# A perceiver block: the last batch's self-attention in two halves of heads, its early routing in quarters of the array, and the experts' residual on VectorE

## The chip, the cores and the metric

The kernel runs on one core of a Trainium2 chip. A core has five engines that run side by side and wait for each other through semaphores: TensorE (PE in the profile; PEld is its loading of weights), VectorE (DVE), ScalarE (ACT), GpSimd (POOL) and SyncE (SP, which here only issues DMAs). The metric is the device time of one execution in microseconds (us), lower is better.

## What is computed

Sixteen batches of 128 rows by 512 columns go through cross-attention to 2048 context rows, self-attention with 16 heads of 32 (causal, half of each head rotated), and a layer of 8 experts of which the first row of each batch chooses two. In short:

```
x = x + softmax(LN(x) ctx^T) ctx                     # cross-attention, LN = layernorm
h = LN(x); q, k, v = h Wq, h Wk, h Wv                # per head, q and k rotated
x = x + (softmax(q k^T * scale + causal) v) Wc       # self-attention
h = LN(x); gates = softmax over the top 2 of h[0] Wr^T
x = x + h + sum over the 2 experts of gate_e * (h A_e^T) B_e^T
```

All data are float32. The choice of experts needs only row 0 of the layernorm after self-attention, and row 0 attends only to itself (the mask is causal), so that its attention output is its own v.

## The kernel before

The kernel is written as four generators per batch, each cut into steps by `yield`, and an order of steps written out by hand.

- `score(b)` (line 260): the first layernorm, its transposes, the scores against the context (`psc`), their maximum (`mx`), the exponentials and sums.
- `attend(b)` (line 323): the weighted sum over the context (`av`), four groups of products; then `x1` and the second layernorm.
- `inner(b)` (line 345): transposes of the layernorm (`hT`), the v projection (`project`), k and q with their rotation (`rotated`, `turned`), `kb` (k spread over a block per head), the comparison (`compare`, products `pss`), softmax in four groups of four heads (`weigh`), the transposed probabilities `pT`, the products with v (`y`, copied to `yT`), and the output projection (`o`), which gives `x2` and the third layernorm.
- `experts(b)` (line 598): transposes (`hT`), the residual `res = x2 + h`, the routing (`shares`, `route`, `gates`), then `mid` and `ffn` and the output.

`early(b)` (line 563) computes the routing of the last batch ahead, from row 0 alone: its v (`v0`), its output row (`o0`), its layernorm, the logits. `route` (line 517) ends in GpSimd's indirect DMAs, which gather the two chosen experts' weights: two into `each` and one into `wb`; GpSimd then copies `each` into `wa`. `each` has one buffer, and so has `res`.

TensorE executes in exactly the order in which the steps issue its products. On VectorE, ScalarE and GpSimd a planner orders the instructions, except for those marked `pinned`, which keep the written order among themselves. All queues run in order once planned.

The main loop (line 708) treats batches 0 to 13. In one round it interleaves `inner(b)`, the score of b + 2, the attend of b + 1 and the experts of b - 1. Transposes go through DRAM there by way of SyncE's queue; the context is loaded through ScalarE's queue, outputs leave through GpSimd's. Lines 756 to 791, after the loop, hold the order of the last two batches, y = 14 and z = 15, whose probabilities are transposed on TensorE instead. In the rotation, VectorE shuffles pairs of rows (line 384), GpSimd multiplies by the sines (line 385), VectorE multiplies by the cosines (line 388) and adds (line 395). The addition reads two SBUF operands, and so does the residual on GpSimd (lines 606 and 608). The products with PE are recorded twice each (a float32 product of 128 columns is two records).

The program prints here what the change touches:

Of the kernel before, what the change touches and what calls it, by code (L numbers as in the profile page):

```python
# [38 lines left out]
C_MIXED = 392  # L39
C_N = 520  # L40
# [6 lines left out]
def constants():  # L47

    c = np.zeros((P, C_N), np.float32)
    c[:, C_MASK : C_MASK + P] = np.where(np.tril(np.ones((S, S), bool)), 0.0, NEG)  # L50
    c[:, C_MIXED : C_MIXED + P] = c[:, C_MASK : C_MASK + P].reshape(P, QD, 4).transpose(0, 2, 1).reshape(P, P)
    inv = (1.0 / np.float32(10000.0) ** (np.arange(0, DE, 2, dtype=np.float32) / DE)).astype(np.float32)
    freqs = np.arange(S, dtype=np.float32)[:, None] * inv[None, :]
    emb = np.concatenate((freqs, freqs), axis=-1)


    cos, sin = np.ones((DH, S), np.float32), np.zeros((DH, S), np.float32)
    cos[DE:] = np.cos(emb).T
    sin[DE:] = np.sin(emb).T * np.tile(np.array([-1.0, 1.0], np.float32), DE // 2)[:, None]
    c[:, C_COS : C_COS + S] = np.tile(cos, (4, 1))  # L60
    c[:, C_SIN : C_SIN + S] = np.tile(sin, (4, 1))
    c[:, C_BLK : C_BLK + 2] = np.arange(P)[:, None] // 32 % 2 == np.arange(2)[None, :]
    at = np.arange(P)
    c[:, C_ONE], c[:, C_TWO] = at < R, at >= R
    c[:, C_ONER], c[:, C_TWOR] = R * (at < R), R * (at >= R)
    c[:, C_RANK], c[:, C_P] = at % R, at
    return c
# [3 lines left out]
def perceiver_block(ctx: ExitStack, tc: tile.TileContext, io: dict, out: bass.AP):  # L71
# [19 lines left out]
    nc.gpsimd.memset(mhalf, -0.5)  # L91

# [252 lines left out]
    def inner(b):  # L345
# [27 lines left out]
        def rotated(n, t):  # L373

            ps = bank(ps_acc, "acc", f"{n}_{b}")
            for m in range(HC):
                for c in range(KC):
                    matmul(
                        ps[:, m * P : (m + 1) * P].rearrange("p (a i) -> p a i", a=4),
# [3 lines left out]
            partner = p1.tile([P, HC, S], F32, tag="partner", name=f"{n}P_{b}")  # L383
            pinned(nc.vector.stream_shuffle(partner.rearrange("p c t -> p (c t)"), ps, PARTNERS))
            nc.gpsimd.tensor_tensor(  # L385
                partner, partner, cst[:, None, C_SIN : C_SIN + S].to_broadcast([P, HC, S]), ALU.mult
            )
            pinned(nc.vector.tensor_tensor(
                t, ps.rearrange("p (c t) -> p c t", c=HC),
                cst[:, None, C_COS : C_COS + S].to_broadcast([P, HC, S]), ALU.mult,  # L390
# [3 lines left out]
        def turned(n, t):  # L394
            pinned(nc.vector.tensor_tensor(t, t, turning[n], ALU.add))  # L395

        kbs, pss, turning = [], [], {}
# [3 lines left out]
        def blocked():  # L401

            turned("k", kT)
            kb = p1.tile([P, HC, 2, S], F32, tag="kb", name=f"kb_{b}")
            for half in range(2):

                nc.scalar.activation(  # L407
                    kb[:, :, half, :].rearrange("p c (q i) -> p c q i", q=4),
                    kT.rearrange("p c (i q) -> p c q i" if mixes else "p c (q i) -> p c q i", q=4),
                    AF.Copy, scale=column(C_BLK + half),  # L410
                )
            kbs.extend(kb[:, c] for c in range(HC))

        def compare():


            pss.extend(
                bank(pool, tag, f"pss_{b}_{tag}_{half}")
                for pool, tag in ((ps_sc, "sc"), (ps_acc, "acc")) for half in range(2)
            )  # L420
            for c, kb in enumerate(kbs):
                for half in range(2):
# [3 lines left out]
                        qT[of, c, :], kb[of].rearrange("p h t -> p (h t)"),  # L426
# [36 lines left out]
        parts += [lambda group=group: weigh(group) for group in range(4)]  # L463

        for part in [project] + parts if b < B - 1 else parts + [project]:
            part()
            yield

        if b >= B - 2:
            flat = att.rearrange("p h t -> p (h t)")  # L470
            for half in range(2):
                transposed(
                    flat[:, half * H // 2 * S : (half + 1) * H // 2 * S], pT[half],
                    f"p_{b}_{half}", True,
                )
                yield
        acc = bank(ps_acc, "acc", f"y_{b}")
        for c in range(HC):
            first = c // 2 * 8 + c % 2 * 2
            for j, n in enumerate((first, first + 1, first + 4, first + 5)):  # L480
                at = c * P + j * DH
                matmul(
                    acc[j * DH : (j + 1) * DH, c * P : (c + 1) * P].rearrange(
                        "p (a i) -> p a i", a=4
                    ),
                    vv[:, at : at + DH], pT[n // 8][:, :, n % 8, :], start=True, stop=True,
                )
        yT = p1.tile([P, HC, S], F32, tag="yT", name=f"yT_{b}")
        nc.scalar.copy(yT, acc.rearrange("p (c t) -> p c t", c=HC))
        yield  # L490
        acc = bank(ps_acc, "acc", f"o_{b}")
        for c in range(HC):
            matmul(acc, yT[:, c, :], w["c"][:, c, :], start=(c == 0), stop=(c == HC - 1))
        x2 = p2.tile([P, D], F32, tag="x2", name=f"x2_{b}")
        nc.vector.tensor_tensor(x2, acc, x1, ALU.add)  # L495
        lasts[b] = (x2, layernorm(x2, f"3_{b}", mix=b >= B - 2))
        yield
# [65 lines left out]
    def early(b):  # L563
# [11 lines left out]
        tr = bank(ps_tr, "tr", f"v0_{b}")  # L575
        for m in range(HC):
            for c in range(KC):
                matmul(
                    tr[:, m : m + 1], w["v"][:, c, m * P : (m + 1) * P], hT[:, 0, c, :1],
                    start=(c == 0), stop=(c == KC - 1),  # L580
                )
        v0 = small(b, KC, "v0")
        nc.vector.tensor_copy(v0, tr[:, :KC])
        yield
        acc = bank(ps_acc, "acc", f"o0_{b}")
        for c in range(KC):
            matmul(acc[:1, :], v0[:, c : c + 1], w["c"][:, c, :], start=(c == 0), stop=(c == KC - 1))
        row = p1.tile([1, D], F32, tag="row", name=f"row_{b}")
# [9 lines left out]
    def experts(b):  # L598
# [5 lines left out]
        res = p1.tile([P, D], F32, tag="res", name=f"res_{b}")  # L604
        if b < B - 2:
            pinned(nc.gpsimd.tensor_tensor(res, x2, h, ALU.add))
        else:
            nc.gpsimd.tensor_tensor(plain(res), plain(x2), mixed(h), ALU.add)
# [15 lines left out]
        nc.scalar.activation(mid, ps[:, :S], AF.Copy, scale=gate)  # L624
        yield
# [142 lines left out]
    step(attend, z)  # L768
    step(inner, y)
    step(attend, z)  # L770
    step(experts, y - 1)
    step(inner, y)
    step(experts, y - 1)
    step(inner, y)
    step(inner, z, 3)
    step(inner, y)
    step(inner, z, 2)
    step(inner, y)
    step(experts, y - 1, 2)
    step(inner, z, 5)  # L780
    step(early, z)
    step(inner, y)
    step(early, z)
    step(inner, z)
    step(experts, y)
    step(early, z)
    step(experts, y, 3)
    step(early, z)
    step(inner, z, 4)
    step(experts, y, 2)  # L790
    step(experts, z, 3)
# [43 lines left out]
```

## Time and profile before

| | |
|---|---|
| median of 3 runs | 845.15 us (843.19 to 848.23) |
| the profiled execution's own time | 850.18 us |
| its span in the profile | 848.1 us |
| PE busy | 809.2 us, 95% of the span |
| VectorE busy | 529.7 us, 62% |
| ScalarE busy | 258.0 us, 30% |
| GpSimd busy | 168.8 us, 20% |
| mean rate of the DMAs | 249 GB/s |
| one round of the loop | 48.83 us |
| last av product of batch 15 ends | 779.20 us |

The span is what lies between the first and the last instruction or transfer that the profile shows; the execution's own time has 2.1 us more around it. A line of a timeline gives start and duration in us, engine, line of the kernel, operation, output and inputs, their shapes, how many, and in brackets the idle time before it and what ended it. L95 is the helper that records every product, L98 the one for transposes, so products are told apart by the names of their tiles. The granted clock is a share of TensorE's full clock.

### The profile page before, as it was taken

The numbers are of one execution on the slowest core, as the hardware profiler recorded it, in microseconds if no ns is written. First come the engines' busy times: TensorE is split into PE (matmuls) and PEld (weight loads), VectorE is DVE, ScalarE is ACT, GpSimd is POOL, SyncE is SP. The second block draws the span as 40 slices with busy tenths as digits, with TensorE's granted clock in tenths as the row PEclk, the third lists the DMA queues.
The fourth block names the chain that finished last, engine by engine and source line by source line (L and its number), as shares of the span: only waits on it lengthen the run. The fifth ranks groups of instructions, "written<-read, shape, count | busy, mean of one in ns | idle before, by whom it ended". The sixth has DMA issues, their size and how long they took to land.

```text
span 848.1 us, 14295 instructions
## 1 busy us (share of the span) xinstructions
PE 809.2 (95%) x5514; PEld 575.3 (68%) x5514; DVE 529.7 (62%) x1204; ACT 258.0 (30%) x763; POOL 168.8 (20%) x232
## 2 busy tenths in 40 slices
PE   6999999999999999999999999999999999998985
PEld 6846775768677675868667576867757686774832
DVE  1454759395675849476584948668593966757541
ACT  1232324151232314133332413223241422324320
POOL 1001011222221212222211122222112222212232
PEclk9999999999999999999999999999999999999897
DMA  9998394958859495876949496684939578450101
GB/s 365 391 353 323 105 378 158 345 219 290 314 181 399 133 363 198 305 287 201 391 141 372 174 325 271 231 355 158 389 144 353 233 252 343 163 224 13 38 21 54
DMA packets 76739, 211.04 MB, mean 249 GB/s; under 512 B 6400, under 2 KB 42624, under 8 KB 60288
## 3 DMA queue, kind: packets, MB, share of 16 engines
q10 hardware_dynamic: 15696, 113.32, 33.5%
q1 hardware_dynamic: 56880, 84.23, 28.2%
q0 software_dynamic: 4096, 12.59, 4.5%
q8 instruction: 43, 0.70, 0.3%
q14 instruction: 24, 0.20, 0.1%
HBM read 180.23 MB, written 29.88 MB: 248 GB/s over the span
## 4 chain that ended last, share of the span: by engine, by line
PE 76%; DVE 14%; POOL 6%; issue 2%; ACT 1%; DMA 0%; DVEq 0%; POOLq 0%; ACTq 0%
PE psc L95 27%; PE av L95 21%; PE o L95 7%; PE v L95 7%; DVE sc L307 3%; DVE qT L395 3%; PE pss_sc L95 2%; POOL kP L385 2%; POOL qP L385 2%; PE y L95 2%; PE ffn L95 2%; PE mid L95 2%; PE pss_acc L95 2%; DVE st L127 1%; DVE x L495 1%
## 5 line engine op out<-in xcount | busy, mean ns | idle before, releaser
L95 PE MATMUL psc<-hT,ctxT 128*128 128x128 f32 x2048 | 237.8, 278 | 1.4 <-ACT hT L173 1.4
L95 PEld LDWEIGHTS psc<-hT,ctxT 128*128 128x128 f32 x2048 | 233.8, 194 | 2.5 <-ACT hT L173 2.0
L95 PE MATMUL av<-ctx,sc 128*128 128x512 f32 x512 | 227.1, 596 | 0.0
L95 PEld LDWEIGHTS av<-ctx,sc 128*128 128x128 f32 x512 | 94.6, 190 | 110.9 <-issue 109.9
L441 ACT ACTIVATE att<-att,nmx 128x128 f32<-128x128 f32 x256 | 98.7, 387 | 102.1 <-DVE nmx L439 102.1
L131 POOL TENSOR_SCALAR rs<-mv 128x1 f32<-128x1 f32 x48 | 11.2, 232 | 445.6 <-DVE mv L129 238.6
L282 ACT COPY sc<-psc 128x512 f32<-128x512 f32 x64 | 37.4, 585 | 139.6 <-PE psc L95 139.6
L310 ACT ACTIVATE sc<-sc 128x512 f32<-128x512 f32 x64 | 40.2, 630 | 90.9 <-DVE sc L307 90.4
L95 PE MATMUL o<-w_c,yT 128*128 128x512 f32 x128 | 61.6, 627 | 4.2 <-issue 4.2
L95 PE MATMUL k<-hT,w_k 128*128 128x128 f32 x512 | 61.6, 280 | 0.7 <-ACT hT L173 0.7
L95 PEld LDWEIGHTS k<-hT,w_k 128*128 128x128 f32 x512 | 60.1, 196 | 1.8 <-ACT hT L173 0.9
L95 PE MATMUL q<-hT,w_q 128*128 128x128 f32 x512 | 59.8, 275 | 0.0
L95 PE MATMUL v<-w_v,hT 128*32 128x512 f32 x512 | 58.7, 592 | 0.9 <-DVE w_v L229 0.9
L95 PEld LDWEIGHTS q<-hT,w_q 128*128 128x128 f32 x512 | 58.5, 192 | 0.0
L285 DVE TENSOR_TENSOR mx<-psc,mx 128x512 f32<-128x512 f32 x32 | 21.6, 676 | 57.3 <-ACT sc L282 57.3
L137 DVE TENSOR_SCALAR h<-x,mv,rs 128x512 f32<-128x512 f32 x48 | 28.2, 587 | 33.1 <-POOL rs L134 33.1
L441 ACT ACTIVATION_READ_ACCUMULATOR att<-att,nmx 128x1 f32 x256 | 47.9, 187 | 0.0
L407 ACT ACTIVATE kb<-kT,cst 128x512 f32<-128x512 f32 x32 | 35.7, 1164 | 37.8 <-DVE kT L395 37.8
L95 PEld LDWEIGHTS o<-w_c,yT 128*128 128x128 f32 x128 | 25.3, 208 | 29.9 <-issue 29.9
L495 DVE TENSOR_TENSOR x<-o,x 128x512 f32<-128x512 f32 x16 | 11.1, 692 | 54.8 <-PE o L95 54.8
L307 DVE TENSOR_TENSOR sc<-sc,spread 128x512 f32<-128x512 f32 x64 | 42.6, 672 | 3.3 <-PE spread L95 3.3
L285 DVE TENSOR_TENSOR mx<-psc,sc 128x512 f32<-128x512 f32 x16 | 11.1, 691 | 53.0 <-ACT sc L282 53.0
(127 smaller groups left out, 933.3 us busy)
## 6 DMA issues: line engine op xcount, KB each, us to landing
ctx<-in_ctx_dram ACTq DMA_DIRECT2D x56, 1024.0 KB
ctxT<-in_ctxT_dram ACTq DMA_DIRECT2D x52, 1024.0 KB
there_p<-pX SPq DMA_DIRECT2D x28, 512.0 KB
pT<-there_p SPq DMA_DIRECT2D x28, 512.0 KB
ctxT<-in_ctxT_dram SPq DMA_DIRECT2D x12, 1024.0 KB
there<-blocks SPq DMA_DIRECT2D x42, 256.0 KB
hT<-there SPq DMA_DIRECT2D x42, 256.0 KB
ctx<-in_ctx_dram SPq DMA_DIRECT2D x8, 1024.0 KB
```

The costliest lines, as they stand in the source:

```text
L95: tc.keep_in_program_order(nc.tensor.matmul(*args, **kwargs))
L131: eps = nc.gpsimd.tensor_scalar_add(rstd, mv[:, 1:2], EPS)
L137: place(nc.vector.tensor_scalar(to, of, mv[:, 0:1], rstd, ALU.subtract, ALU.mult))
L282: nc.scalar.copy(sc[:, v], ps)
L285: nc.vector.tensor_tensor(mx, ps, mx if v > 1 else sc[:, 0], ALU.max)
L307: nc.vector.tensor_tensor(sc[:, v], sc[:, v], spread[:, None, :S].to_broadcast([P, 4, S]), ALU.add)
L310: nc.scalar.activation(sc[:, v], sc[:, v], AF.Exp)
L385: nc.gpsimd.tensor_tensor(partner, partner, cst[:, None, C_SIN : C_SIN + S].to_broadcast([P, HC, S]), ALU.mult)
L395: pinned(nc.vector.tensor_tensor(t, t, turning[n], ALU.add))
L407: nc.scalar.activation(kb[:, :, half, :].rearrange("p c (q i) -> p c q i", q=4), kT.rearrange("p c (i q) -> p c q i" if mixes else "p c (q ...
L441: nc.scalar.activation(att[:, i, :], att[:, i, :], AF.Exp, bias=nmx[:, i : i + 1], accum_out=sm[:, i : i + 1],)
L495: nc.vector.tensor_tensor(x2, acc, x1, ALU.add)
```

## The change

It has five parts.

1. The residual `res` of every batch moves from GpSimd to VectorE and is issued after `mid` instead of ahead of the routing.
2. For the last batch k and q are computed for two halves of the heads (column chunks 0, 1 and 2, 3), each with its own rotation; the sines are multiplied by VectorE there. Comparison, softmax, the products with v and the output projection run by halves too (`here` and `there`).
3. For the last batch's early routing, `v0` and `o0` are computed by quarters: each of four products takes one quarter of the sum and writes one strip of 32 rows, with weights of 32 columns and 512 moving columns. The strips are added by a product with `C_SEL`, a new column of the constants that is 1 in every 32nd row. `padded`, zero but for one column, holds row 0's v for the second of these.
4. The tail's order of steps is new: batch 13's routing stands ahead of batch 15's last av group, both halves of batch 14's probabilities and its y around batch 15's transposes, batch 14's output and batch 13's experts among the halves of batch 15.
5. `kb` and `yT` are allocated at the start of a batch's self-attention instead of where they are written.

```
-        def rotated(n, t):
+        def rotated(n, t, chunks=slice(0, HC), sines=nc.gpsimd):
...
-            for m in range(HC):
+            for m in range(chunks.start, chunks.stop):
...
-            nc.gpsimd.tensor_tensor(
-                partner, partner, cst[:, None, C_SIN : C_SIN + S].to_broadcast([P, HC, S]), ALU.mult
+            sines.tensor_tensor(
+                partner, partner, cst[:, None, C_SIN : C_SIN + S].to_broadcast(some), ALU.mult
             )
...
+            parts = [
+                lambda: k_of(here), lambda: q_of(here), lambda: k_of(there),
+                lambda: compare((0,)), lambda: both(0), lambda: q_of(there),
+                lambda: compare((1,)), lambda: both(2), project,
+                lambda: probabilities(0), lambda: weighted(here), lambda: output(here),
+                lambda: probabilities(1), lambda: weighted(there), lambda: output(there),
+            ]
...
-        tr = bank(ps_tr, "tr", f"v0_{b}")
-        for m in range(HC):
+        def quarters(columns, weights, name, room):
+
+            ps = bank(ps_tr, "tr", f"{name}_{b}")
             for c in range(KC):
-                matmul(
-                    tr[:, m : m + 1], w["v"][:, c, m * P : (m + 1) * P], hT[:, 0, c, :1],
-                    start=(c == 0), stop=(c == KC - 1),
-                )
-        v0 = small(b, KC, "v0")
-        nc.vector.tensor_copy(v0, tr[:, :KC])
-        yield
-        acc = bank(ps_acc, "acc", f"o0_{b}")
-        for c in range(KC):
-            matmul(acc[:1, :], v0[:, c : c + 1], w["c"][:, c, :], start=(c == 0), stop=(c == KC - 1))
-        row = p1.tile([1, D], F32, tag="row", name=f"row_{b}")
+                matmul(ps[c * QD : (c + 1) * QD, :], columns(c), weights[:, c, :], start=True, stop=True)
+            t = p1.tile([P, 4, KC, QD], F32, tag=room, name=f"{name}s_{b}")
+            t = t.rearrange("p a n j -> p (a n j)")
+            nc.vector.tensor_copy(t, ps)
+            return t
+
+        t = quarters(lambda c: hT[:, 0, c, :], w["v"], "v0", "blocks_1")
+        yield
+        tr = bank(ps_tr, "tr", f"v0t_{b}")
+        for m in range(KC):
+            matmul(tr[:, m : m + 1], t[:, m * P : (m + 1) * P], column(C_SEL), start=True, stop=True)
+        nc.vector.tensor_copy(padded[:, :, 0], tr[:, :KC])
+        t = quarters(lambda c: padded[:, c, :], w["c"], "o0", "blocks_2")
+        yield
+        acc = bank(ps_tr, "tr", f"o0t_{b}")
+        matmul(acc[:1, :], column(C_SEL), t, start=True, stop=True)
...
-        res = p1.tile([P, D], F32, tag="res", name=f"res_{b}")
-        if b < B - 2:
-            pinned(nc.gpsimd.tensor_tensor(res, x2, h, ALU.add))
-        else:
-            nc.gpsimd.tensor_tensor(plain(res), plain(x2), mixed(h), ALU.add)
...
         nc.scalar.activation(mid, ps[:, :S], AF.Copy, scale=gate)
+        res = p1.tile([P, D], F32, tag="res", name=f"res_{b}")
+        if b < B - 2:
+            pinned(nc.vector.tensor_tensor(res, x2, h, ALU.add))
+        else:
+            nc.vector.tensor_tensor(plain(res), plain(x2), mixed(h), ALU.add)
```

The tail's order after the change, from batch 15's third group of av products on; step n of a generator is named by what it issues:

```
attend z (av group 2)      experts 13 (route)        inner y (weigh 2)
attend z (av group 3, x1)  inner y (weigh 3)         experts 13 (gates)
inner y (both halves of probabilities)               inner z (transposes)
inner y (y)                inner z (k here, q here, k there, compare here, weigh 0 and 1, q there)
early z (v0)               experts 13 (mid, res)     inner y (o)
experts 13 (ffn)           inner z (compare there, weigh 2 and 3)
early z (v0 added up, o0)  inner z (v projection)    early z (o0 added up, row)
experts y (transposes)     inner z (probabilities here)   experts y (shares)
early z (row transposed, shares)   experts y (route)  inner z (y here)
early z (route, gates)     experts y (gates)
inner z (o here, probabilities there, y there, o there)
experts y (mid, res)       experts z (transposes)    experts y (ffn)
experts z (mid, res, ffn)
```

## The prediction

> **What bounds the kernel.** I read the page first (TensorE, PE, is busy 95% of the span, all other engines under 63%), then the waits of PE, then one round of the loop, then the end.
>
> The list of who waited for whom (us in total, times, longest) names PE's one frequent wait:
>
> ```profile
> PE pss_sc L95 <- DVE qT L395: 12.8, 14, 1.2
> ```
>
> The busy time of one round (stretch, length, then PE, PEld, DVE, ACT, POOL, granted clock, DMA share, GB/s) agrees: PE is idle 0.90 us of 48.83, and the DMA engines are not full.
>
> ```profile
> 652.13:700.96 48.83, 47.93 (x336) 34.33 (x329) 32.92 (x75) 15.32 (x46) 10.43 (x14) 1.00 0.71 261
> ```
>
> The timeline of a round shows where that idle time comes from:
>
> ```profile
> 761.99 3.60 PE L95 MATMUL av<-ctx,sc 128*128 128x512 f32 x8
> ...
> 763.30 1.27 POOL L385 TENSOR_TENSOR qP<-qP,cst 128x512 f32<-128x512 f32 x1 [1.74 <-DVE qP L384]
> ...
> 764.53 1.26 POOL L606 TENSOR_TENSOR res<-x,h 128x512 f32<-128x512 f32 x1
> ...
> 764.60 1.74 DVE L395 TENSOR_TENSOR qT<-qT,qP 128x512 f32<-128x512 f32 x1 [0.88 <-POOL qP L385]
> ...
> 766.48 1.14 PE L95 MATMUL pss_sc<-kb,qT 64*128 64x256 f32 x8 [0.90 <-DVE qT L395]
> ```
>
> qT's addition takes 1.74 us beside GpSimd's residual, which started 0.07 us earlier; kT's, the same shape and line, takes 0.69 at 761.59 with GpSimd free. PE waits for the difference.
>
> The end is another regime. PE's own timeline:
>
> ```profile
> 782.72 0.66 PE L98 MATMUL tr<-ident,h 128*128 128x128 f32 x4 [2.48 <-DVE g_blocks L531]
> 784.05 5.47 PE L95 MATMUL k<-hT,w_k 128*128 128x128 f32 x32 [0.67 <-ACT hT L173]
> ...
> 799.50 4.97 PE L95 MATMUL v<-hT,w_v 128*128 128x1 f32 x32
> 804.34 5.78 PE L95 MATMUL o<-w_c,yT 128*128 128x512 f32 x8
> 810.05 3.17 PE L95 MATMUL o<-w_c,g_v 128*1 128x512 f32 x7
> ...
> 828.33 5.40 PE L95 MATMUL o<-w_c,yT 128*128 128x512 f32 x8 [4.24 <-issue]
> ```
>
> The same k product takes 3.74 elsewhere and the same o product 3.60: after idle stretches, and after the products with one column (v at 799.50), the clock is halved. In windows of 2 us it is 0.50 at 802 to 808 and at 830 to 832. The 4.24 at 828.33 is ScalarE's copy yT, which began 3.6 us after its product had ended, released by nothing the trace names.
>
> The last piece is a chain through the single buffer res:
>
> ```profile
> 837.97 0.67 POOL L633 DMA_DIRECT2D out_dram<-res  x1 [1.58 <-DVE res L632]
> ...
> 840.47 1.51 POOL L608 TENSOR_TENSOR res<-x,h 128x512 f32<-128x512 f32 x1 [1.84 <-DMA out_dram<-res]
> ...
> 842.02 0.42 DVE L632 TENSOR_TENSOR res<-ffn,res 128x256 f32<-128x256 f32 x1 [4.35 <-POOL res L608]
> ```
>
> Batch 15's residual waits until batch 14's output has left the buffer.
>
> **The Trainium skill.** "SBUF — State Buffer", section "Who interferes with whom": a VectorE instruction with two SBUF inputs is blocked by a GpSimd instruction that reads SBUF until that one is done. The trace agrees (1.74 against 0.69). "TensorE: Matmul & The Clock Gate", Part 1: a window of some 3.4 us of idleness halves the clock for at least one such window; the trace agrees (slow from about 784.6 to 788). Its Part 3: products in different column strips of the array run side by side; batch 14's v product shows it (32 records of 512 columns in 3.62 us, 0.11 each, against 0.43 for a full-width one). "TensorEngine Tiling (Array Packing)", "Instruction Overhead": a product of one column isn't proportionally cheaper; here 32 records of one column took 4.97 us.
>
> **Part 1, the residual moved to VectorE.** Fourteen additions (L606) leave GpSimd. qT then ends at 764.60 + 0.69 = 765.29, and with the 0.14 us from its end to pss's start PE could go on at 765.43; av ends at 765.59. The wait goes whole, with 0.16 to spare; kb ends at 763.72 and is not next. VectorE gains 14 additions of 0.69, behind ScalarE's mid. There (735.5 to 746.4) it has two additions of 0.69 and waits of 2.4 to 3.8 us for ScalarE's copies; its next urgent result, mx, is ready at 747.9 and used at 751.0. Hidden; without that cover 0.69 x 14 = 9.7 us. The round shrinks by 2% with DMA at 0.71, so no transfer takes the wait's place. Gain **12.8 us** (bounds: 0, if something else is late at once, to 12.8).
>
> **Part 2, the tail.** I add it up from the end of the last av product, 779.20: 68.9 us to the end of the span. The constant column and the memset at the start are hidden by the first loads.
>
> *To the first k product.* In the new order batch 13's route product (lg, 0.23) and perhaps 0.3 of waiting for g_part stand ahead of the last av group, since VectorE made g_part at 775.99 and PE would be there at about 775.7: 0.5. Then batch 15's layernorm, 3.52 from av's end to its transposes (782.72), covers both halves of batch 14's probabilities (16 transposes, 2.02 in the row at 820.27). The gather of batch 13, three GpSimd DMAs of about 1 us, now comes earlier and can sit in front of the layernorm's two small GpSimd steps: 0 to 0.7, I take 0.3. Transposes 0.66, y 1.0, which covers ScalarE's copy of hT. Sum 0.5 + 3.5 + 0.3 + 0.7 + 1.0 = **6.0**.
>
> *From there to the end of the v projection.* k and q in four halves: 4 x 1.79 = 7.2. VectorE's four steps on half the columns cost about 0.35 each in a chain (0.42 is the 256-column row at 747.16), 1.4; they lie beside the next half. The sine product on VectorE instead of GpSimd (1.27) needs no crossing. qT's first half is ready 1.6 after its product, k's second half covers 1.79. Compare 1.9. v0 by quarters: 8 records of 0.107, 0.9; its transposes of one column 1.0 (eight records in tr_row, 1.05); o0 by quarters 0.9. They replace 4.9 and 3.6. mid 0.9, o of batch 14 3.45 at full clock (5.65 before), ffn 0.9, project 3.4. Between v0's transposes and o0's quarters PE waits for a small VectorE copy; in VectorE's queue that can stand behind the second half's mask additions and maxima (four of 0.65): 0.35 to 2.6, I take 1.5; behind it on PE stand o0, the v projection and all that follows. The clock may still halve at the first k (its wait is 1.5 instead of 2.5, but transposes lie about it): 0 to 1.9, I take 0.95. Sum 7.2 + 1.9 + 2.8 + 0.9 + 3.45 + 0.9 + 3.4 + 1.5 + 0.95 = **23.0**.
>
> *From the projection to the end.* o0's sum over quarters 0.9; row, layernorm, row transposed: 3.5 (814.35 to 817.83), PE having only batch 14's transposes and the first probabilities beside it; tr_row 1.05; route products and y of the first half 1.0; yT's copy 0.25; o half 1.7; transposes 0.95; copy pT 0.7; y half 0.5; copy 0.45; o half 1.7: 12.7. Layernorm to transposes 3.5, transposes 0.66: 16.9. Now ffn of batch 14 comes after these transposes (before, it stood ahead): 0.86, VectorE's sum 0.8, GpSimd's issue 0.95, landing 1.84, residual 0.7 (on VectorE now; behind its wait stand only the last two sums), then as before 6.1 from the first half's sum (842.02) to the end: 28.1. mid and ffn of batch 15 are ready at 19.9, in its shade. GpSimd's gathers of two batches took 10.4 us (821.82 to 832.22) behind one buffer; they now start at about 7.3 and end at 17.7, while the layernorm needs GpSimd at about 14.5: 0 to 3, I take 1.0. Half clock at the end, 0 to 1, I take 0.5. Sum **29.6**.
>
> Tail 6.0 + 23.0 + 29.6 = 58.6 instead of 68.9: gain 10.3.
>
> **Sum.** 12.8 + 10.3 = 23.1: the profiled span of 848.1 becomes 825.0. That execution took 850.18 (2.1 outside the span), 5.0 above the median of 845.15. Its unnamed 4.24 us stall may be why. If the median runs have it too, 845.15 - 23.1 = 822.1; if not, the gain is 18.9 and the time 826.3. I take the middle, **824 us**.
>
> **Rivals.**
> 1. The loop's wait goes but the tail gives nothing, because VectorE's queue, the gathers and the clock take up what the routing saves. For it: all bounds of part 2 at their bad ends cost 0.4 + 1.1 + 0.95 + 2 + 0.5 = 5.0 more, and the stall's 4.24 can be absent from the median. Against it: 8.5 us of routing products shrink to 3.6 (with the sum). 845.15 - 12.8 = 832.4.
> 2. In the loop kb or VectorE's own order replaces the wait, and only the tail gains: 845.15 - 10.3 = 834.9. Against it: the 0.16 us to spare at qT, and kb ready 1.9 us before av's end.
> 3. Slower, by the half clock. Smaller pieces with a wait between each could keep the windows idle enough for half clock from k to the end. The PE work there is some 34 us at full clock and would cost 34 more, 1.5 of it counted: -23.1 + 32.5 = +9, 854. It decides from 24 us of extra on, so most of the tail must be slow. For it: clock shares of 0.66 and 0.50 in the tail's slices. Against: the long one-column product that led to the longest slow stretch is gone.
>
> **Numbers.** Forecast 0.68 (own range 815 to 830), rival 1 0.16, rival 2 0.08, slower 0.04; 0.04 is left for gains that cancel to within 0.5%, about what a measurement here tells from no change. Faster 0.92, same 0.04, slower 0.04. Range: with every bound at its good end (0.3 + 0.3 + 1.15 + 0.95 + 1.0 + 0.5 = 4.2 off) and the stall in the median 817.9, and 813 where some 5 us of the waits that I added in a row lie beside each other; up to 835 for rivals 1 and 2.
>
> **What would show it.** Right: no PE wait for qT in the loop, qT at 0.69, a round of 47.9; v0 in about 0.9; batch 15's residual on VectorE waiting for the output DMA. Wrong: PE waiting for kb or g_part each round; idle PE over 2.6 us before o0; k and o records at double length through the tail.

## The result, and the profile after

The change makes the kernel faster, by a third of what was forecast. The timed runs of the two kernels, side by side:

| | before | after |
|---|---|---|
| median of 5 runs | 845.15 us (843.19 to 848.23) | 838.20 us (836.97 to 838.36) |
| ratio of the times, 95% interval | | 0.9909 [0.9884, 0.9935] |
| profiled execution's own time, span | 850.18, 848.1 us | 836.97, 835.2 us |
| one round of the loop | 48.83 us | 47.86 us |
| last av product of batch 15 ends | 779.20 us | 766.1 us |
| from there to the end of the span | 68.9 us | 69.1 us |

7 us gained instead of 21. The two profiles alone would say 13.2 (850.18 - 836.97); the profiled execution of before was a long one, and that of after the shortest of its five.

**The loop did what was forecast.** The list of who PE waited for, after (us in total, times, longest), has no long entry for qT, which had 12.8 us before:

```profile
PE tr L103 <- DVE h L142: 14.9, 3, 6.6
PE o L100 <- DVE padded L635: 2.9, 1, 2.9
PE tr_row L100 <- DVE hrow_row L142: 2.0, 1, 2.0
...
PE pss_sc L100 <- DVE qT L403: 0.4, 2, 0.2
```

The busy time of one round of the loop, after (stretch, length, then PE, PEld, DVE, ACT, POOL, clock, DMA share, GB/s):

```profile
642.48:690.34 47.86, 47.86 (x334) 34.16 (x331) 32.48 (x76) 15.32 (x46) 9.22 (x13) 1.00 0.72 265
```

PE is busy in all of it. The timeline of that round, after, shows qT's addition at 0.69 us (1.74 before), done before the av products end, and pss directly behind them:

```profile
653.45 3.60 PE L100 MATMUL av<-ctx,sc 128*128 128x512 f32 x8
...
656.07 0.69 DVE L403 TENSOR_TENSOR qT<-qT,qP 128x512 f32<-128x512 f32 x1 [0.89 <-POOL qP L394]
...
656.98 1.13 PE L100 MATMUL pss_sc<-kb,qT 64*128 64x256 f32 x8
```

**The tail gained nothing against the first profile of before.** What heads the list of waits now lies there: h, padded, hrow_row (of the 14.9 us for h, 6.6 are the very first wait of the kernel, 6.5 before). PE's timeline from the end of the last av product on, after:

```profile
772.53 1.08 PE L103 MATMUL tr<-ident,h 128*128 128x128 f32 x4 [4.64 <-DVE h L142]
773.54 1.94 PE L100 MATMUL y<-pT,vv 128*32 128x128 f32 x32
775.41 2.82 PE L100 MATMUL k<-hT,w_k 128*128 128x128 f32 x16
...
781.95 1.13 PE L100 MATMUL pss_sc<-kb,qT 64*128 64x256 f32 x8 [0.15 <-DVE qT L403]
...
796.82 1.30 PE L100 MATMUL o<-w_c,padded 128*32 128x512 f32 x8 [2.90 <-DVE padded L635]
797.88 5.14 PE L100 MATMUL v<-w_v,hT 128*32 128x512 f32 x32
...
810.89 3.78 PE L100 MATMUL o<-w_c,yT 128*128 128x512 f32 x4
...
823.98 0.66 PE L103 MATMUL tr<-ident,h 128*128 128x128 f32 x4 [3.71 <-DVE h L142]
```

Idle stretches of 4.64, 2.90 and 3.71 us (and 2.03 for hrow_row, ahead of 807.35), with slow products behind them or soon after: the four transposes at 772.53 take 0.66 us at 823.98, y takes 1.08 at full clock in kernels shown below, the v projection 3.62, and the half output product (3.78 at 810.89) 1.98 at 817.40. The windows of the same stretches, after, give the granted clock in the third column from the right:

```profile
772.00:780.00 8.00, 7.47 (x70) 6.70 (x71) 2.01 (x6) 1.17 (x2) 0.00 (x0) 0.68 0.01 2
780.00:796.00 16.00, 13.41 (x83) 8.76 (x81) 14.32 (x33) 5.26 (x21) 1.47 (x3) 1.00 0.04 17
796.00:804.00 8.00, 7.18 (x44) 1.93 (x45) 4.15 (x10) 3.78 (x17) 0.00 (x0) 0.79 0.01 2
804.00:815.00 11.00, 8.95 (x49) 6.02 (x48) 5.76 (x34) 2.50 (x6) 3.44 (x5) 0.69 0.07 18
```

Why the first h was late stands in GpSimd's timeline, after. Its layernorm step `rs` needs `mv`, which VectorE had finished at 768.27 (768.09 + 0.18):

```profile
765.92 1.09 POOL L581 DMA_INDIRECT each<-in_A_dram,g_blocks  x1 [14.16 <-DVE g_blocks L576]
767.31 0.99 POOL L581 DMA_INDIRECT each<-in_A_dram,g_blocks  x1 [0.30 <-issue]
768.60 0.96 POOL L586 DMA_INDIRECT wb<-in_BT_dram,g_rows  x1 [0.30 <-issue]
770.12 0.61 POOL L591 COPY wa<-each 128x512 f32<-128x512 f32 x1 [0.57 <-DMA each<-in_A_dram,g_blocks]
770.71 0.23 POOL L136 TENSOR_SCALAR rs<-mv 128x1 f32<-128x1 f32 x1
```

The gather of batch 13, its wait for the data and the copy into `wa` stand in front; `rs` is 2.4 us late. The three issues by themselves, which end at 769.56, make up 1.3 of it. The same happens once more at the end: the `mv` of batch 15's last layernorm is ready at 821.06 (820.88 + 0.18), its `rs` starts at 822.26, directly behind the second `wa` copy of the last two batches.

Why padded was late stands in VectorE's timeline, after:

```profile
792.97 1.29 DVE L441 TENSOR_TENSOR att<-pss_acc,cst 128x512 f32<-128x512 f32 x2
794.87 0.74 DVE L142 TENSOR_SCALAR h<-x,mv,rs 128x512 f32<-128x512 f32 x1 [0.61 <-POOL rs L139]
795.44 1.26 DVE L447 TENSOR_REDUCE nmx<-att 128x4 f32<-128x512 f32 x2
796.61 0.16 DVE L635 COPY padded<-v0t 128x4 f32<-128x4 f32 x1
```

A copy of 0.16 us stands behind the second half's mask additions and maxima and batch 14's layernorm, 3.6 us in all; v0t's products had ended at 793.92.

The end itself is the chain through `res` as before, with the addition on VectorE (the timeline of the end, after):

```profile
827.06 0.67 POOL L685 DMA_DIRECT2D out_dram<-res  x1 [3.91 <-DVE res L684]
829.57 1.07 DVE L676 TENSOR_TENSOR res<-x,h 128x512 f32<-128x512 f32 x1 [2.81 <-DMA out_dram<-res]
830.74 0.76 DVE L684 TENSOR_TENSOR res<-ffn,res 128x256 f32<-128x256 f32 x2
```

### The profile page after: what moved, and what is told of

Same layout as the page of the kernel before. It is cut to its first block, busy times and chain, and to the rows that moved or that the text cites. A ratio compares the mean times of both kernels' runs of the same rounds, so it can differ in the third digit from the quotient of the medians.

```text
span 835.2 us, 14284 instructions
## 1 busy us (share of the span) xinstructions
PE 804.6 (96%) x5500; PEld 569.6 (68%) x5500; DVE 529.9 (63%) x1234; ACT 258.9 (31%) x766; POOL 146.1 (17%) x215
## 4 chain that ended last, share of the span: by engine, by line
PE 89%; DVE 5%; POOL 2%; ACT 1%; issue 1%; DMA 1%; DVEq 0%; POOLq 0%; ACTq 0%
PE psc L100 28%; PE av L100 25%; PE v L100 7%; PE o L100 6%; PE k L100 6%; PE q L100 6%; PE y L100 2%; PE pss_sc L100 2%; PE pss_acc L100 1%; PE mid L100 1%; PE ffn L100 1%; ACT att L449 1%; DMA each<-in_A_dram,g_blocks 1%; PE lg L100 0%; PE tr_m L103 0%
## 5 line engine op out<-in xcount | busy, mean ns | idle before, releaser
L100 PE MATMUL v<-w_v,hT 128*32 128x512 f32 x520 | 60.5, 605 | 0.9 <-DVE w_v L234 0.9
L100 PE MATMUL o<-w_c,yT 128*128 128x512 f32 x128 | 59.7, 609 | 0.5 <-ACT yT L493 0.5
L290 DVE TENSOR_TENSOR mx<-psc,mx 128x512 f32<-128x512 f32 x32 | 21.6, 676 | 55.6 <-ACT sc L287 55.6
L415 ACT ACTIVATE kb<-kT,cst 128x512 f32<-128x512 f32 (+1 forms) x34 | 36.2, 1111 | 43.0 <-DVE kT L403 43.0
L454 DVE TENSOR_TENSOR att<-att,rsm 128x512 f32<-128x512 f32 x64 | 43.3, 677 | 0.7
L447 DVE TENSOR_REDUCE nmx<-att 128x4 f32<-128x512 f32 x64 | 41.6, 672 | 0.0
```

The lines of the kernel that those rows point to most:

```text
L100: tc.keep_in_program_order(nc.tensor.matmul(*args, **kwargs))
L290: nc.vector.tensor_tensor(mx, ps, mx if v > 1 else sc[:, 0], ALU.max)
L415: nc.scalar.activation(kb[:, chunks, half, :].rearrange("p c (q i) -> p c q i", q=4), kT[:, chunks, :].rearrange("p c (i q) -> p c q i" if ...
L447: nc.vector.tensor_reduce(nmx[:, hs], att[:, hs, :], AX.X, ALU.max, negate=True)
L454: nc.vector.tensor_tensor(att[:, hs, :], att[:, hs, :], rsm[:, hs, None].to_broadcast([P, 4, S]), ALU.mult)
```

## The experiments

The theory after this reading: the residual and the loop gave the whole gain; the new tail costs time, because (a) GpSimd's gathers stand in front of layernorms, (b) VectorE's queue holds up padded, and (c) TensorE's clock is halved behind the idle stretches that (a) and (b) make. The rivals: the tail's pieces (quarters, halves) are dear in themselves; or the profile of before was atypical and the tail was never as long as it looked. Gains below are the ratio's distance from 1 times the median of before in the same series (845.83, 846.61 or 845.64 us).

### The kernel before, profiled and timed once more

No edit.

> The kernel before, unedited, for a second profile. Theory A (its first profile, 5 us above the median, held a stall that most executions don't have): the gap of 4.2 us ahead of batch 15's output product is absent or under 1 us, the span is about 843 and the tail from the end of the last av product about 64 to 65 us. Theory B (the stall is part of the kernel): the gap is there again, the tail is 69 us. Time 845 either way.

Measured: ratio 0.9997 [0.9981, 1.0014], as it has to be, but a profile 6.5 us shorter: span 841.6, of which 62.4 follow the end of the last av product (779.18), not 68.9. PE's timeline of this second execution of before:

```profile
799.49 3.73 PE L95 MATMUL v<-hT,w_v 128*128 128x1 f32 x32
803.08 3.68 PE L95 MATMUL o<-w_c,yT 128*128 128x512 f32 x8
...
821.47 3.70 PE L95 MATMUL o<-w_c,yT 128*128 128x512 f32 x8 [0.74 <-ACT yT L489]
```

In the first these three were 4.97, 5.78 and 5.40, with 4.24 us of idleness ahead of the last. So neither the half clock behind the one-column product nor the stall comes with every execution. The stall is in no other profile: two kernels below that keep this tail wait 0.77 and 0.76 us there. The half clock does come back: the o product behind the one-column v takes 5.38 us in one kernel below and 4.85 in another, and 3.68 and 3.60 in two more. The median of before, 845.15, less the 2.1 outside the span, leaves 63.9 us for its tail (843.05 - 779.18), near the second profile. That is an estimate: it takes the time up to the tail as the two profiles show it, where the last av product ends at 779.20 and 779.18.

### The residual alone, and the rest alone

The first kernel is the one before with the residual moved, the second the one after with it moved back:

```
# residual alone (on the kernel before)
-        res = p1.tile([P, D], F32, tag="res", name=f"res_{b}")
-        if b < B - 2:
-            pinned(nc.gpsimd.tensor_tensor(res, x2, h, ALU.add))
-        else:
-            nc.gpsimd.tensor_tensor(plain(res), plain(x2), mixed(h), ALU.add)
         if b not in routes:
...
         nc.scalar.activation(mid, ps[:, :S], AF.Copy, scale=gate)
+        res = p1.tile([P, D], F32, tag="res", name=f"res_{b}")
+        if b < B - 2:
+            pinned(nc.vector.tensor_tensor(res, x2, h, ALU.add))
+        else:
+            nc.vector.tensor_tensor(plain(res), plain(x2), mixed(h), ALU.add)
# tail alone: the same lines the other way, on the kernel after
```

> The kernel before with the residual alone moved to VectorE behind mid; the tail's order, the halves and the quarters stay as before. Theory A (the loop gives all 12.8 us and the rest of the change costs some 6): about 832 to 833, ratio about 0.985, faster than the changed kernel by 5 to 6 us. Theory B (median against median the loop gives only about 7 and the tail nothing): about 838, as the changed kernel.

> The changed kernel with the residual put back on GpSimd at its old place, so that the tail's new order, halves and quarters stand alone. Theory A: about 851, slower than before by some 6 us (ratio 1.007). Theory B: about 845, ratio 1.000. The forecast on record would have it at 835.

Measured: residual alone 830.69 us, ratio 0.9840 [0.9813, 0.9866], a gain of 13.5; tail alone 852.54 us, ratio 1.0085 [1.0062, 1.0107], a loss of 7.2. The product 0.9840 x 1.0085 = 0.9924 lies within the interval of the whole change, so the two add up. **One part of the change makes the kernel faster, the rest makes it slower**; a kernel with the residual alone is faster than the changed one. In the tail alone PE waits 4.72 us for h at 786.58 and 2.91 for padded at 811.02: the same two stretches as in the changed kernel, without the residual's move.

### The residual moved in the loop only

```
-        if b < B - 2:
-            pinned(nc.gpsimd.tensor_tensor(res, x2, h, ALU.add))
-        else:
+        if b >= B - 2:
+            res = p1.tile([P, D], F32, tag="res", name=f"res_{b}")
             nc.gpsimd.tensor_tensor(plain(res), plain(x2), mixed(h), ALU.add)
...
+        if b < B - 2:
+            res = p1.tile([P, D], F32, tag="res", name=f"res_{b}")
+            pinned(nc.vector.tensor_tensor(res, x2, h, ALU.add))
```

> The kernel before with the residual moved to VectorE in the loop's fourteen batches only; batches 14 and 15 keep it on GpSimd. Theory A (the loop's waits for qT are worth 12.8 us, and the residual's place in the last two batches some 2 more): ratio 0.985, about 12.8 below before, 2 us slower than the residual moved in all batches. Theory B (all of the 15.1 us of that kernel come from the loop): 15 below before.

Measured: 834.16 us, ratio 0.9859 [0.9839, 0.9879]: 11.9 us, 10.2 to 13.6. The forecast of 12.8 for the loop lies in it. The 1.6 us between this kernel and the residual alone are less than the intervals of the two. Its tail is that of the kernel before, and PE's timeline has the half clock of the first profile of before behind the one-column product again, for the o product alone (3.68 in the second profile):

```profile
785.84 3.73 PE L95 MATMUL v<-hT,w_v 128*128 128x1 f32 x32
789.43 5.38 PE L95 MATMUL o<-w_c,yT 128*128 128x512 f32 x8
```

### Batch 13's gather behind the layernorm

On the changed kernel, only the order of steps in the tail:

```
     step(attend, z)
-    step(experts, y - 1)
     step(inner, y)
     step(attend, z)
+    step(experts, y - 1)
     step(inner, y)
```

> The changed kernel with batch 13's route step put back behind batch 15's second layernorm, so that GpSimd runs the layernorm's two small steps ahead of the gather. Theory A (the layernorm stood behind the gather's three DMAs and the wait for them, and the long idle stretch halved the clock): the wait for the layernorm's h falls from 4.6 to 1.5 to 2 us, y and k come at full clock, 4 to 6 us faster than the changed kernel, about 833. Theory B (GpSimd's order doesn't matter, something later waits anyway): within 1 us of 838.

Measured: 830.67 us, ratio 0.9828 [0.9802, 0.9854] against 0.9909, 6.8 us better than the changed kernel. GpSimd's timeline of this kernel has the layernorm first:

```profile
766.84 0.22 POOL L136 TENSOR_SCALAR rs<-mv 128x1 f32<-128x1 f32 x1 [15.49 <-DVE mv L134]
767.15 0.57 POOL L139 TENSOR_TENSOR rs<-rs,mhalf 128x1 f32<-128x1 f32 x1
768.82 1.10 POOL L581 DMA_INDIRECT each<-in_A_dram,g_blocks  x1 [1.10 <-DVE g_dn L602]
```

and PE's timeline a shorter wait with full clock behind it:

```profile
768.63 0.63 PE L103 MATMUL tr<-ident,h 128*128 128x128 f32 x4 [1.54 <-DVE g_blocks L576]
769.19 1.08 PE L100 MATMUL y<-pT,vv 128*32 128x128 f32 x32
770.20 2.05 PE L100 MATMUL k<-hT,w_k 128*128 128x128 f32 x16
```

Wait and clock move together here, so this run can't say which of them was dear.

### The clock alone: products that fill the wait

On the changed kernel, five products that nothing reads, put between batch 14's transposed probabilities and batch 15's transposes. The gather stays ahead of the layernorm:

```
     step(inner, y, 2)
+    warm = bank(ps_sc, "sc", "warm")
+    for _ in range(5):
+        matmul(warm, ident, w["c"][:, 0, :], start=True, stop=True)
     step(inner, z)
```

> The changed kernel with five products that nothing reads (some 4.3 us of TensorE work) put between batch 14's transposed probabilities and batch 15's transposes, where TensorE waits 4.6 us for the layernorm. The late layernorm stays. Theory A (that stretch halves the clock, and this is a cost of its own beside the wait): transposes, y and the first k come at full clock (1.08 to 0.66, 1.94 to 1.08, 2.82 to 1.95), 1.5 to 2.5 us faster than the changed kernel, about 836. Theory B (all of the cost is the wait): 838, no change.

Measured: 832.90 us, ratio 0.9852 [0.9827, 0.9876], 4.8 us better than the changed kernel. PE's timeline of this kernel:

```profile
767.78 4.46 PE L100 MATMUL warm<-w_c,ident 128*128 128x512 f32 x10
772.64 0.63 PE L103 MATMUL tr<-ident,h 128*128 128x128 f32 x4 [0.40 <-DVE h L142]
773.19 1.08 PE L100 MATMUL y<-pT,vv 128*32 128x128 f32 x32
774.20 2.05 PE L100 MATMUL k<-hT,w_k 128*128 128x128 f32 x16
...
779.98 1.13 PE L100 MATMUL pss_sc<-kb,qT 64*128 64x256 f32 x8 [0.15 <-DVE qT L403]
...
807.66 3.28 PE L100 MATMUL o<-w_c,yT 128*128 128x512 f32 x4 [0.23 <-ACT yT L493]
```

The transposes start as late as in the changed kernel (772.64 against 772.53), but they, y and k are at full clock, and pss starts 2.0 us earlier (779.98 against 781.95). So the half clock behind the wait is a cost of its own. How the 6.8 us that the early gather cost divide between wait and clock isn't shown. Of the 4.1 us between the two profiled spans (835.2 and 831.1) these 2.0 lie behind the filled wait, within the 1.5 to 2.5 expected; the others come mostly some 25 us later, at the row's transposes, y and o of batch 15's first half (o 3.28 against 3.78), and nothing in the trace ties those to the filled wait. The intervals of the two runs, 2 us to each side, are too wide for the difference of 4.8 and 6.8.

### padded ahead of the second half's softmax

On the kernel with the later gather, one exchange:

```
-    step(inner, z, 2)
-    step(early, z)
     step(inner, z)
     step(early, z)
+    step(inner, z, 2)
+    step(early, z)
```

> As route_late, and batch 15's second pair of softmax groups is issued behind the early routing's second step, so that VectorE's small copy into padded stands ahead of most of the mask additions and maxima. Theory A (TensorE's 2.9 us wait for padded is VectorE's queue, and the halved clock in the v projection follows from it): the wait falls under 1 us, 2 to 4 us faster than route_late's 830.7, about 828. Theory B (the softmax that is pushed back is late next, for the probabilities): 830 to 831.

Measured: 827.26 us, ratio 0.9768 [0.9741, 0.9795] against 0.9828: 5.1 us by the ratios, 3.4 by the medians. PE's timeline of this kernel:

```profile
788.84 1.06 PE L100 MATMUL o<-w_c,padded 128*32 128x512 f32 x8 [0.26 <-DVE padded L635]
789.72 3.62 PE L100 MATMUL v<-w_v,hT 128*32 128x512 f32 x32
...
798.00 1.71 PE L100 MATMUL tr_row<-ones,hrow_row 1*128 1x1 f32 x8 [2.06 <-DVE hrow_row L142]
```

2.9 us of waiting became 0.26, and the v projection behind it runs at full clock. It does so, at 3.62, in all three profiles of quarters with the short wait, and takes 4.32 to 5.67 in the four with the long one.

### Columns instead of quarters

`v0` and `o0` in the form of the kernel before, all else left, once on the kernel with the later gather and once on that of the section before with the last copy on ScalarE (below):

```
-        t = quarters(lambda c: hT[:, 0, c, :], w["v"], "v0", "blocks_1")
+        tr = bank(ps_tr, "tr", f"v0_{b}")
+        for m in range(HC):
+            for c in range(KC):
+                matmul(tr[:, m : m + 1], w["v"][:, c, m * P : (m + 1) * P], hT[:, 0, c, :1],
+                    start=(c == 0), stop=(c == KC - 1),
+                )
+        v0 = small(b, KC, "v0")
+        nc.vector.tensor_copy(v0, tr[:, :KC])
         yield
-        t = quarters(lambda c: padded[:, c, :], w["c"], "o0", "blocks_2")
+        acc = bank(ps_acc, "acc", f"o0_{b}")
+        for c in range(KC):
+            matmul(acc[:1, :], v0[:, c : c + 1], w["c"][:, c, :], start=(c == 0), stop=(c == KC - 1))
```

> As route_late, with the early routing's v0 and o0 computed as in the kernel before (products of one column, then of one row), in the same places. Theory A (the wait for padded and the added steps eat what the quarters save on TensorE): within 1.5 us of route_late's 830.7. Theory B (the quarters are worth the 4.9 us of the prediction): about 835.5.

> As route_padded_wa, with v0 and o0 by columns and rows as in the kernel before. Theory A (once the wait for padded is gone the quarters save what their shorter TensorE time says, 3.6 + 3.5 against some 4.2 with the small wait): the quarters' kernel is 2 to 3 us faster, so this one is about 828. Theory B (the products of the early routing are covered by other waits of the tail): within 1 us of route_padded_wa's 825.6.

Measured: 828.26 us, ratio 0.9792 [0.9767, 0.9817], against 0.9828 with quarters; and 826.92 us, 0.9771 [0.9749, 0.9793], against 0.9768 with quarters. The quarters, priced at a saving of 4.9 us, are worth nothing that these runs can tell from zero. Part of the reason can be read in the two timelines. With columns:

```profile
800.06 1.02 PE L100 MATMUL tr_row<-ones,hrow_row 1*128 1x1 f32 x8 [1.03 <-DVE g_share L551]
```

With quarters, same order:

```profile
797.42 1.02 PE L100 MATMUL tr_row<-ones,hrow_row 1*128 1x1 f32 x8 [2.07 <-DVE hrow_row L142]
```

One us of what the quarters save is waited for at once, behind the row's layernorm. And the price itself was taken from one execution where v0 ran partly at half clock: v0 in columns was 4.97 there and 3.73 in the second profile of before. What takes the remainder isn't settled; the profiles of the second pair differ by 3.1 us in span (825.0 and 821.9) where the timed ratios don't differ, so single profiles don't decide it. Some 1.7 of the 3.1 are the half clock behind the one-column product in that one execution (mid 1.61 and o 4.85 against 1.16 and 3.60).

### The last copy on ScalarE, and filling at two more places

The last batch's copy of `each` into `wa` on ScalarE, so that batch 15's layernorm is not behind it on GpSimd; then the same with products that nothing reads, two after the first half's probabilities and three ahead of batch 15's last transposes:

```
# both
-        nc.gpsimd.tensor_copy(
+        (nc.scalar.copy if b == B - 1 else nc.gpsimd.tensor_copy)(
# the second alone; warm(n) issues n of the products shown above
     step(inner, z)
+    warm(2)
     step(experts, y)
...
+    warm(3)
     step(experts, z)
```

> As route_padded, and the copy of batch 15's gathered weights is made by ScalarE, so that GpSimd doesn't wait for the gather ahead of the last layernorm's two small steps. Theory A (in the changed kernel that layernorm stood some 1.2 us behind this copy, on the path to the end): 1 us faster than route_padded, more where the idle stretch gets short enough for the clock. Theory B (the path to the end runs through batch 14's output and the single res buffer, or through the copy itself): same as route_padded.

> As route_padded_wa, with products that nothing reads in the two longest waits of TensorE that are left (two ahead of the transposed row, three ahead of batch 15's last transposes). Theory A (the half clock after those waits still costs): output by halves at full clock, 1 to 3 us faster, 823 to 824. Theory B (the stretch behind them is bound by the gather and the output's DMA, not by TensorE): within 1 us of route_padded_wa.

Measured: 825.59 us, ratio 0.9768 [0.9742, 0.9794], the same ratio as without the copy's move; and 824.21 us, 0.9741 [0.9723, 0.9759]. The first has no effect that can be measured, the second's 2.3 us against the first lie within the intervals. Before the last transposes the second kernel has no idle stretch, and the products from there to the end run at full clock. But ffn behind them takes 1.02 in the first kernel too, behind 2.59 us of waiting (1.55 after), so the trace shows no gain of the filling here. PE's timeline of the second kernel:

```profile
809.53 2.74 PE L100 MATMUL warm<-w_c,ident 128*128 128x512 f32 x6
812.30 0.66 PE L103 MATMUL tr<-ident,h 128*128 128x128 f32 x4
```

This last kernel beats both: 21.9 us under the one before (20.4 to 23.4), 14 under the changed one. It is also 8.4 us under the residual alone (0.9741 against 0.9840, intervals apart), and the kernel with padded ahead is 6.1 under it. So the new tail's pieces, as a whole, aren't dear in themselves: with the waits gone the new tail beats the old one. No run has the new order without the halves, so their part isn't shown.

### What sets the end

The stretch from GpSimd's first gather for batches 14 and 15 to the end of the span changes far less than the tail does, which runs from 57.3 us (fastest) to 70.5 (tail alone):

| kernel | first gather | end of span | between |
|---|---|---|---|
| before, second profile | 818.46 | 841.6 | 23.1 |
| after | 811.74 | 835.2 | 23.5 |
| tail alone | 825.76 | 850.6 | 24.8 |
| residual alone | 805.53 | 827.1 | 21.6 |
| gather later | 806.45 | 828.9 | 22.5 |
| and padded earlier | 802.64 | 826.1 | 23.5 |
| fastest | 801.08 | 822.5 | 21.4 |

The kernels not listed lie between 21.4 and 23.0, but for the first profile of before, with its stall: 26.3. Halves of heads at the end of the tail hardly shorten it. GpSimd needs about 10.5 us for the gathers of two batches through the one buffer `each` (811.74 to 822.28 after), and where it also makes the copies, the layernorm that starts the last chain stands behind them. It does so in the second profile of before too, where PE waits 3.06 us for that h. With the last copy on ScalarE that is no longer so: in the fastest kernel `rs` waits 1.48 us for `mv`, and the stretch is 21.4 all the same. What a change of order gains is, in these profiles, mostly what it gains up to the gather's start. What sets the rest stays open; a kernel with a second buffer for `each` wasn't tried.

## Why the prediction was right in the loop and wrong in the tail

**Part 1, "Gain 12.8 us": right.** The wait went whole, the round became 47.86, the last av product ends 13.1 earlier, and moved in the loop alone the residual is worth 11.9 (10.2 to 13.6). The mechanism was the one read from the trace and from the Trainium skill ("SBUF — State Buffer", "Who interferes with whom"): qT's addition takes 0.69 once no GpSimd addition lies beside it.

**Part 2, "58.6 instead of 68.9: gain 10.3": wrong, and in sign.** Measured against before as it usually runs, the tail loses 7.2 us. Stage by stage of the sum:

| stage, from the end of the last av product | forecast | after |
|---|---|---|
| to the first k product | 6.0 | 9.3 |
| to the end of the v projection | 23.0 | 27.4 |
| to the end | 29.6 | 32.4 |

The forecast's 6.0 holds 0.5 for batch 13's route product, which lies ahead of the end of the av products and so isn't in the 9.3. Four terms of the sum failed.

1. *"The gather of batch 13 … can sit in front of the layernorm's two small GpSimd steps: 0 to 0.7, I take 0.3."* It was 2.4. Of three issues of about 1 us, all ahead of `rs`, only 0.3 was taken, and they alone made 1.3; that the copy into `wa` follows in the same queue, waits 0.57 for the data and takes 0.61, was not counted. At the end the same collision was priced 1.0 and measured 1.2.
2. *Half clock: "0 to 1.9, I take 0.95" at the first k, "0 to 1, I take 0.5" at the end.* This is the largest miss. Row by row after, against the full-clock rows of the other kernels: transposes 0.42 more, y 0.86, k 0.77, o0 0.24, v projection 1.52, tr_row 0.43, two route products 0.42, first half of y 0.44, first half of o 1.80; 6.9 in sum, not 1.45 (ffn and mid at the end, 1.55 and 1.91 against 1.02 and 1.16, aren't in it).

   Of the 6.9, 2.05 stand behind the wait for h and 1.76 behind that for padded, and there the runs with the wait filled or gone show the cause. The last 1.80 stay, nearly whole, in the repaired kernels too, so the idle stretches don't explain them; and the rows between come and go at the same wait of 2.0 us.

   The Trainium skill's statement ("TensorE: Matmul & The Clock Gate", Part 1) was cited with the forecast, and the trace agrees in part: clock 0.68 in the window behind the idle 4.64 us. But the v projection is slow behind 2.90 us too, and in the profile of before, which the forecast took as agreeing, the longest stretch ahead of the slow k was 2.48; both are shorter than the page's window of about 3.4 us. There the measurement decides, and what counts beside idleness no run shows. The forecast priced the clock at two places, the first k and the end, while the plan made idle stretches at four. Rival 3 described this mechanism, with a price of 32.5; the real one was smaller and ended the tail's gain without turning the whole into a loss.
3. *padded: "0.35 to 2.6, I take 1.5."* 2.90, above its upper end: batch 14's layernorm (0.74, after 0.61 of waiting for GpSimd) stands in VectorE's queue between the mask additions and the maxima and was left out of the list.
4. *"They replace 4.9 and 3.6."* The 4.9 was read with the clock partly halved; at full clock it is 3.73. The replacement took what it should (1.06, 1.05, 1.30 and 1.02 us), but the exchange is worth nothing measurable.

Terms 1 to 3 account for 2.3 + 5.5 + 1.4 = 9.2 of the 10.5 us by which the tail of the profiled execution exceeds the forecast; the rest is spread over small steps. In the profile of the fastest kernel, which has both orders repaired, the tail takes 57.3 us, near the 58.6 of the sum. So it was the waits and the clock behind them that were priced wrong, more than the products.

**The base: "I take the middle".** Half of the stall's 4.24 us was counted as part of the usual run. The second profile shows 0.74 in its place, and v0 and o at full clock; by the estimate from the median the usual tail is some 64 us and not 68.9. With the forecast's own 58.6 this gives a gain of 12.8 + 5.3 = 18.1, 827 us: about 3 us of the error are the base, 11 are the tail. That the long one-column product leads to the half clock was read from that execution alone; of the six profiles with this product, three have the half clock (o behind it 5.78, 5.38, 4.85) and three don't (3.60 to 3.68). It was also the argument against rival 3.

**Rival 1** (the loop alone, 832.4) came nearest in its mechanism: VectorE's queue, the gathers and the clock did take up the saving. Its bound, all bad ends together 5.0 more, was too small, because the bounds for the waits were set without the clock behind them.

Of the signs named ahead, those of being right came in the loop (47.9, qT 0.69) and for v0 (1.06) and the residual waiting for the output's DMA (2.81); those of being wrong came in the tail, in part: 2.90 idle ahead of o0 as named, but double length only for the first half of o (3.78 against 1.98), with v at 5.14 and k at 2.82 some 40% long.

## What to carry to other kernels

A step that is moved ahead brings everything that its engine runs in order with it: list the issue, the wait for the data and the copy behind it, and ask which two-instruction layernorm now stands behind them. Where TensorE's work is cut into small pieces with a wait between them, price the wait together with the clock behind it; here the clock cost no less than the waits, and five products that nothing reads gave 4.8 us back, of which the trace shows 2.0 directly behind them. And take the sum for a tail from more than one execution, since one profile can hold a stall that the median doesn't have.

## What the runs showed of the hardware that was not expected

- The clock behind the same products of the same program differs between executions: v0 in columns 4.97 and 3.73 us, the output product behind it 5.78 and 3.68 (5.38 and 4.85 in two other kernels).
- The first half of batch 15's o stays slow in the kernels with the change's tail, 3.28 to 3.78 us in all nine profiles, 3.38 in the fastest and 3.78 after, and the half clock follows no idle stretch in the fastest: ahead of it stand waits of 0.35 and 0.23, and 1.8 us of products with one element or eight columns. What the clock answers to there stays open. The window of it, in the fastest kernel (columns as above):

```profile
802.00:804.00 2.00, 2.00 (x5) 0.86 (x4) 0.89 (x8) 0.00 (x0) 1.40 (x3) 0.50 0.23 66
```

- PE's idle 4.24 us ahead of batch 15's o, where ScalarE's copy yT began 3.6 us after its product had ended (the trace gives "remote" as the releaser and no instruction), was 0.74 in the second execution of the same program.
- The residual takes 0.67 us on VectorE where its operands are contiguous, but 1.07 to 1.12 in the rearranged form of the last two batches; on GpSimd 1.26 and 1.51.
